# Gated cross-attention on one core: how the context matrix is loaded and transposed, and how W_mem's columns are read

## The chip, the core and the metric

The kernel runs on one core of a Trainium2 chip. The metric is the device time of one execution in microseconds. Before the change it is 992.16 us, the median of three runs (992.13 to 992.58). Engines are named as in the profile: PE is the tensor engine (PEld its weight loads), DVE the vector engine, ACT the scalar engine, POOL GpSimd, SP the engine that here only issues DMAs.

## The reference

Inputs are `x` (8 x 1024 x 1024), a context `mem` (8 x 64 x 512), `W_mem` (1024 x 512), `W_gate` (1024 x 2048), a bias and a norm weight, all float32. Cut to what is computed:

```python
memory_proj = jnp.einsum('bme,de->bmd', memory, W_mem)
scores = jnp.einsum('bnd,bmd->bnm', hidden_states, memory_proj) / jnp.sqrt(jnp.float32(D))
attn = jax.nn.softmax(scores, axis=-1)
memory_context = jnp.einsum('bnm,bmd->bnd', attn, memory_proj)
gate_input = jnp.concatenate([hidden_states, memory_context], axis=-1)
gate = jax.nn.sigmoid(jnp.einsum('bnf,df->bnd', gate_input, W_gate) + b_gate)
fused = hidden_states + gate * memory_context
return _rmsnorm(fused, norm_w)
```

The change concerns the first line alone: the product of the context with W_mem. Here B = 8, M = 64 and E = 512, so the context is 512 rows (`BM`) of 512 numbers; D = 1024.

## The kernel before, in words

The kernel has an opening, which is the part that matters here, and a long main loop.

**The order of the work.** Nearly every instruction is kept in program order on its engine (`pin`, line 88). A helper `load` (line 96) issues a DMA on SP, so all of these stand in one queue. A DMA or an instruction waits until the tile that it writes is free and the tiles that it reads are written; tiles of one tag share a buffer.

**The opening.** PE first multiplies a tile of zeros nine times (`pz`, lines 118 to 120). Meanwhile the context comes into two tiles `memq`, 256 rows each, in eight DMAs of pieces of 512 bytes: each DMA fills 32 partitions with a quarter of the columns (`load_mem`, lines 130 to 132). With the columns spread over four groups of partitions in this way, a block-wise transpose of 32x32 on DVE gives the full transpose; `transpose_mem` (lines 190 to 196) does this in four instructions, reading every fourth element (`chunks`, line 106), into `memT`, which has the 512 columns on partitions in four chunks of 128 and the 512 rows along the free dimension. W_mem arrives transposed in `wm` (line 128): two quarters by ACT's queue (line 137), the last half by SP (line 139). ACT then copies it into `wmp` (lines 199 to 209), which turns columns that lie eight elements apart into contiguous ones, in eight copies of 128x512.

**The product.** Eight PSUM banks `pm` (lines 226 to 228) take D in eight chunks `j`, each 128 rows of D by 512 context rows, and lines 229 to 239 accumulate over the four chunks `k` of E. For k = 0 the product is done in two halves of 256 columns, so that it can begin with the first half of the context; for the other k each matmul has 512 columns. A float32 matmul appears as two records of PE, each with a weight load of its own. DVE copies the eight banks to `mpT` (line 241), and PE goes on with the context's share of the gate, `pg` (lines 433 to 454: eight tiles, each of eight matmuls of 512 columns), fed by the eight tiles `w2`.

**Queues around it.** SP issues, in this order: the context, the last half of W_mem, the eight `w2` tiles, the bias, the two `w1` tiles, the first block of x (`load_xq(0)`, line 242, four DMAs), the norm weight, then 16 stores of the transposed projection to `mgd` (line 253) and four to `mpd` (line 260), and later the stores of the `pg` stages (line 441). `xq` has the same buffer as `wm` (tag "xq"). At most eight of these DMAs are under way at once. The first reader of `xq` is `transpose_x` in the list `first` (line 425), which is begun in the fifth `pg` tile (line 446).

**The main loop.** For each of 16 blocks of 512 rows of x, seven outer products of a Strassen-like scheme, each in seven inner products (`kA` to `kF`), with scores, softmax and gate between them by slots. The change doesn't touch it.

Of the kernel before, what the change touches and what calls it, by code (L numbers as in the profile page):

```python
# [8 lines left out]
F32 = mybir.dt.float32  # L9
# [6 lines left out]
P = 128  # L16
# [4 lines left out]
def tile_gated_cross_attention_rmsnorm(  # L21
# [41 lines left out]
    nc = tc.nc  # L63
    B, N, D = x.shape
    M, E = mem.shape[1:]
# [3 lines left out]
    BM = B * M  # L69
    KD = D // P  # L70
    KE = E // P
    H = 512
    C = 256
# [7 lines left out]
    apool = ctx.enter_context(tc.tile_pool(name="apool", bufs=1))  # L81
    rot = ctx.enter_context(tc.tile_pool(name="rot", bufs=2))
    small = ctx.enter_context(tc.tile_pool(name="small", bufs=1))
    ps = ctx.enter_context(tc.tile_pool(name="ps", bufs=1, space=PSUM))
    ps_ctx = ctx.enter_context(tc.tile_pool(name="ps_ctx", bufs=2, space=PSUM))
    dram = ctx.enter_context(tc.tile_pool(name="dram", bufs=1, space=DRAM))

    pin = tc.keep_in_program_order

    def mm(o, lhsT, rhs, start, stop):  # L90
        pin(nc.tensor.matmul(o, lhsT, rhs, start=start, stop=stop, skip_group_check=True))  # L91
# [4 lines left out]
    def load(o, i):  # L96
        pin(nc.sync.dma_start(o, i))

    def t4k(pool, shape, tag, name):
        return pool.tile(shape, F32, tag=tag, name=name)  # L100

    def rows_by_chunk(w, n):

        return w.rearrange("(p j) f -> p j f", j=n)

    def chunks(t, n):

        return t.rearrange("p s e -> p (s e)").rearrange("p (m j) -> p j m", j=n)
# [3 lines left out]
    def bank(n, shape, name):  # L112
        return ps.tile(shape, F32, tag=banks[n % 5], name=name)
# [1 line left out]

    zeros = t4k(small, [P, C], "junk", "zeros")
    pin(nc.vector.memset(zeros, 0.0))
    pz = ps.tile([P, C], F32, tag="sc", name="pz")
    for _ in range(9):
        mm(pz, zeros[:, :P], zeros, True, True)  # L120

    memq = [t4k(rot, [P, BM // 64, E // 4], "l2", f"memq{i}") for i in range(2)]
    memr = mem.rearrange("b m e -> (b m) e").rearrange(
        "(g s c) (i e) -> g i c s e", g=2, c=32, i=4
    )
    wm = t4k(xqpool, [P, KE, D], "xq", "wm")

    def load_mem(g):  # L130
        for i in range(4):
            load(memq[g][32 * i : 32 * (i + 1), :, :], memr[g, i])

    wmr = rows_by_chunk(w_mem_t, KE)
    load_mem(0)
    for k in range(2):
        pin(nc.scalar.dma_start(wm[:, k, :], wmr[:, k, :]))
    load_mem(1)
    load(wm[:, 2:, :], wmr[:, 2:, :])
    w2r = rows_by_chunk(w_gate_t[D:, :], KD)  # L140
    w2 = []
    for k in range(KD):
        t = t4k(*((gpool, [P, D], "gate") if k < 7 else (apool, [P, D], "s4")), f"w2_{k}")
# [36 lines left out]
    ident = const.tile([P, P], F32, name="ident")  # L180
# [6 lines left out]
    mgd = dram.tile([2, BM, D], F32, name="mgd")  # L187
    memT = [t4k(apool, [P, 2, BM], f"a1{i + 1}", f"memT{i}") for i in range(2)]

    def transpose_mem(g, i):  # L190
        pin(
            nc.vector.transpose(
                memT[i][:, :, g * (BM // 2) : (g + 1) * (BM // 2)],
                chunks(memq[g], KE)[:, 2 * i : 2 * i + 2],
            )
        )


    wmp = []
    for k in range(KE):  # L200
        t = t4k(apool, [P, KD, P], ("a21", "a22", "s1", "s2")[k], f"wmp{k}")
        for j in (0, KD // 2):
            pin(
                nc.scalar.copy(
                    t[:, j : j + KD // 2, :],
                    chunks(wm[:, k : k + 1, :], KD)[:, j : j + KD // 2],
                )
            )
        wmp.append(t)

    for i in range(2):
        for g in range(2):
            transpose_mem(g, i)

    mpT = [
        t4k(rot, [P, 2, BM], tag, f"mpT_{tag}_{i}")
# [6 lines left out]


    mpq = [t4k(apool, [P, 4, Q4], f"a{i}{j}", f"mpq{i}{j}") for i in (1, 2) for j in (1, 2)]
    pm = [bank(j, [P, BM], f"pm{j}") for j in range(5)]
    pm += [ps_ctx.tile([P, BM], F32, tag="ctx", name=f"pm{j}") for j in (5, 6)]
    pm += [ps.tile([P, BM], F32, tag="sc", name="pm7")]
    for k in range(KE):

        for cols in ([slice(0, BM // 2), slice(BM // 2, BM)] if k == 0 else [slice(0, BM)]):
            for j in range(KD):
                mm(
                    pm[j][:, cols],
                    wmp[k][:, j, :],
                    memT[k // 2][:, k % 2, cols],
                    k == 0 and cols.start == 0,
                    k == KE - 1,
                )
    for j in range(KD):  # L240
        pin(nc.vector.tensor_copy(mpT[j // 2][:, j % 2, :], pm[j]))
    load_xq(0)
# [189 lines left out]
    done, n = 0, 0  # L432
    for h in range(2):
        cols = slice(h * H, (h + 1) * H)
# [349 lines left out]
```

## Time and profile before

| what | value |
|---|---|
| median of three runs | 992.16 us (992.13 to 992.58) |
| the profiled execution's own time | 992.3 us |
| its span | 990.5 us, mean granted clock 0.995 |
| busy: PE, DVE, POOL, ACT | 972.9, 812.2, 688.7, 327.9 us |
| chain that ended last: PE, DVE, DMA | 95%, 2%, 1% |
| first record of `pm`, first record of `pg` | 11.43, 40.70 us |
| ACT copies `wmp<-wm` (8) | 8.4 us |
| DVE transposes `memT<-memq` (4) | 4.2 us |

The profile shows one execution. The span goes from its first to its last instruction; 1.8 us of the execution's time lie around it. A group of instructions is written as line, engine, operation, output<-inputs by the program's names, shapes and count, then busy time and the mean of one in ns, then the idle time of the engine just before them and what ended it. The matmuls and DMAs have the lines of their helpers (91 and 97), so one goes by the names of tiles. The chain of work is followed back from the last instruction to what released each step. PE's records overlap each other, since matmuls are pipelined: what counts is the distance from start to start.

### The profile page before, as it was taken

The page shows a single profiled execution, that of the slowest core. Times are in us where ns is not written, and L with a number is a line of the kernel's source. Part 1 is how long each engine was busy: PE and PEld are TensorE (multiplying, and loading weights), DVE is VectorE, ACT ScalarE, POOL GpSimd, SP SyncE. Part 2 cuts the span into 40 slices and gives each one's busy share as a digit, 9 for nine tenths or more (in the row PEclk, how much of TensorE's full clock was granted, in tenths as well). Part 3 has the DMA queues.
Part 4 walks back from the last instruction along what each step waited for, and adds up shares of the span by engine and source line. Part 5 has one row for each costly group of instructions (what it writes and reads, how often), then busy time and mean ns, then how long its engine had stood idle before and what let it go on. Part 6 is the DMA issues. An engine that isn't in the chain of part 4 may idle for free.

```text
span 990.5 us, 14285 instructions
## 1 busy us (share of the span) xinstructions
PE 972.9 (98%) x4962; PEld 768.9 (78%) x4962; DVE 812.2 (82%) x1491; ACT 327.9 (33%) x596; POOL 688.7 (70%) x851
## 2 busy tenths in 40 slices
PE   7999999999999999999999999999999999999995
PEld 5445888888788888888888888888887888888873
DVE  1587787979898897979788897979798988979787
ACT  3000215234343416143333425152343434161444
POOL 0002677878788787878697886878787887878772
PEclk9999999999999999999999999999999999999998
DMA  9951628192825547291926456381927365381612
GB/s 313 308 184 47 114 40 185 43 197 81 153 93 120 136 106 161 60 195 65 175 91 118 118 127 140 82 195 43 186 81 142 114 127 118 89 188 60 176 65 85
DMA packets 70792, 126.76 MB, mean 128 GB/s; under 512 B 12480, under 2 KB 49344, under 8 KB 70336
## 3 DMA queue, kind: packets, MB, share of 16 engines
q1 hardware_dynamic: 61792, 93.34, 35.1%
q0 software_dynamic: 8640, 31.46, 17.1%
q10 hardware_dynamic: 288, 1.05, 0.4%
q8 instruction: 39, 0.64, 0.3%
q14 instruction: 33, 0.27, 0.1%
HBM read 85.98 MB, written 39.85 MB: 127 GB/s over the span
## 4 chain that ended last, share of the span: by engine, by line
PE 95%; DVE 2%; DMA 1%; issue 0%; ACT 0%; POOL 0%; SPq 0%; DVEq 0%; ACTq 0%
PE kA L91 19%; PE pc L91 12%; PE kE L91 11%; PE kF L91 10%; PE kD L91 10%; PE kC L91 10%; PE kB L91 10%; PE psT L91 6%; PE pg L91 6%; PE pm L91 3%; DVE gate L94 1%; DMA memq<-in_mem 1%; DVE gate L598 0%; PE pa L395 0%; PE sc L369 0%
## 5 line engine op out<-in xcount | busy, mean ns | idle before, releaser
L94 POOL TENSOR_TENSOR gate<-gate,u 128x256 f32<-128x256 f32 x336 | 270.6, 836 | 122.5 <-DVE u L94 120.5
L94 POOL TENSOR_TENSOR l<-a 128x256 f32<-128x256 f32 x128 | 129.1, 1009 | 153.7 <-PE pg L91 89.4
L520 ACT ACTIVATE gate<-gate 128x512 f32<-128x512 f32 x128 | 79.0, 629 | 400.5 <-DVE gate L94 400.5
L301 DVE STREAM_TRANSPOSE a<-xq 128x512 f32<-128x512 f32 x128 | 137.8, 1099 | 0.0
L91 PE MATMUL pc<-mg,attnT 64*128 64x256 f32 x512 | 127.4, 389 | 0.0
L549 DVE SCALAR_TENSOR_TENSOR gate<-gate,ss,nw_sb 128x512 f32<-128x512 f32 x120 | 125.2, 1053 | 1.1
L91 PE MATMUL kB<-it,l 128*128 128x256 f32 x448 | 115.0, 379 | 0.0
L91 PE MATMUL kD<-it,l 128*128 128x256 f32 x448 | 115.0, 379 | 0.0
L91 PEld LDWEIGHTS pc<-mg,attnT 64*128 64x128 f32 x512 | 90.6, 186 | 29.7 <-issue 21.2
L91 PE MATMUL kA<-w,a 128*128 128x256 f32 x384 | 98.7, 379 | 0.4 <-ACT u L664 0.4
L91 PEld LDWEIGHTS kD<-it,l 128*128 128x128 f32 x448 | 85.1, 190 | 11.6
L91 PEld LDWEIGHTS kB<-it,l 128*128 128x128 f32 x448 | 85.1, 190 | 11.6
L94 DVE TENSOR_TENSOR gate<-gate,pc 128x512 f32<-128x512 f32 x128 | 87.2, 681 | 5.9 <-ACT gate L520 5.9
L664 ACT COPY u<-kA 128x256 f32<-128x256 f32 x112 | 40.5, 362 | 138.4 <-PE kA L91 136.4
L91 PEld LDWEIGHTS kA<-w,a 128*128 128x128 f32 x384 | 71.6, 190 | 10.2 <-ACT u L664 0.8
L94 POOL TENSOR_TENSOR l<-s 128x256 f32<-128x256 f32 x96 | 75.6, 787 | 1.8 <-PE kF L91 1.8
L94 DVE TENSOR_TENSOR u<-u,kB 128x256 f32<-128x256 f32 x112 | 45.6, 407 | 30.3 <-PE kB L91 26.3
L91 PE MATMUL kE<-it,a 128*128 128x256 f32 x256 | 69.0, 392 | 0.0
L91 PE MATMUL kA<-t,s 128*128 128x256 f32 x256 | 67.4, 386 | 0.0
L91 PE MATMUL kC<-w,l 128*128 128x256 f32 x256 | 65.7, 379 | 0.0
L91 PE MATMUL kF<-w,l 128*128 128x256 f32 x256 | 65.7, 379 | 0.0
L534 ACT ACTIVATE junk<-gate 128x1024 f32<-128x1024 f32 x60 | 63.5, 1058 | 1.5 <-DMA gate<-in_x 0.4
(105 smaller groups left out, 1959.8 us busy)
## 6 DMA issues: line engine op xcount, KB each, us to landing
xq<-in_x SPq DMA_DIRECT2D x64, 512.0 KB, 10.1
gate<-in_x POOLq DMA_DIRECT2D x60, 512.0 KB, 9.0
out<-gate SPq DMA_DIRECT2D x60, 512.0 KB, 2.6
w<-in_w_gate_t SPq DMA_DIRECT2D x8, 512.0 KB, 9.5
w<-in_w_gate_t SPq DMA_DIRECT2D x2, 2048.0 KB, 17.2
mg<-mgd SPq DMA_DIRECT2D x16, 256.0 KB, 4.2
mgd<-mpq SPq DMA_DIRECT2D x16, 128.0 KB, 2.6
mgd<-g SPq DMA_DIRECT2D x8, 256.0 KB, 2.1
```

What stands on the lines that cost most here:

```text
L91: pin(nc.tensor.matmul(o, lhsT, rhs, start=start, stop=stop, skip_group_check=True))
L94: pin(eng.tensor_tensor(o, a, b, op))
L301: nc.vector.transpose(A[key][:, :, r * P : (r + 1) * P], chunks(xq[q][:, 4 * t : 4 * t + 4, :], KD)[:, half * KH : (half + 1) * KH],)
L520: pin(nc.scalar.activation(g, g, AF.Sigmoid))
L534: nc.scalar.activation(junk, O[q, t], AF.Square, accum_out=ss[:, t % 2 : t % 2 + 1])
L549: nc.vector.scalar_tensor_tensor(g[:, cols], g[:, cols], rstd[:, t % 2 : t % 2 + 1], nw_sb[:, cols], ALU.mult, ALU.mult,)
L664: pin(nc.scalar.copy(p1, kb["A"]))
```

## The change

The context comes in two plain loads of 256 rows, two rows of 2 KB to a partition, both on SP. It is transposed on PE, 16 blocks of 128x128: the block, with every fourth element of a row, is the stationary operand, the identity the moving one. The blocks go to four PSUM banks `pt`, one for each chunk of E; DVE and ACT copy them to `memT` in turn, 256 columns at a time. The four banks are those that the product takes last (`pm4` to `pm7`). After the transposes of each half of the context come that half's products of chunk k = 0 for the first four chunks of D; when both halves are done, the other four chunks follow for k = 0 with 512 columns, and then the rest.

W_mem's columns, eight elements apart, are read from `wm` as the stationary operand as they lie; `wmp` and its copies are gone. With that `wm` is read until the product's last matmul. ACT's queue issues only W_mem's first quarter; the second goes to SP behind the context. The warm-up has five products of zeros instead of nine, in another bank.

```diff
@@ -115,27 +115,19 @@
     zeros = t4k(small, [P, C], "junk", "zeros")
     pin(nc.vector.memset(zeros, 0.0))
-    pz = ps.tile([P, C], F32, tag="sc", name="pz")
-    for _ in range(9):
+    pz = bank(0, [P, C], "pz")
+    for _ in range(5):
         mm(pz, zeros[:, :P], zeros, True, True)

-    memq = [t4k(rot, [P, BM // 64, E // 4], "l2", f"memq{i}") for i in range(2)]
-    memr = mem.rearrange("b m e -> (b m) e").rearrange(
-        "(g s c) (i e) -> g i c s e", g=2, c=32, i=4
-    )
+    memr = mem.rearrange("b m e -> (b m) e").rearrange("(g s p) e -> g p s e", g=2, p=P)
+    memq = [t4k(rot, [P, 2, E], "l2", f"memq{i}") for i in range(2)]
     wm = t4k(xqpool, [P, KE, D], "xq", "wm")
-
-    def load_mem(g):
-        for i in range(4):
-            load(memq[g][32 * i : 32 * (i + 1), :, :], memr[g, i])
-
     wmr = rows_by_chunk(w_mem_t, KE)
-    load_mem(0)
-    for k in range(2):
-        pin(nc.scalar.dma_start(wm[:, k, :], wmr[:, k, :]))
-    load_mem(1)
+    pin(nc.scalar.dma_start(wm[:, 0, :], wmr[:, 0, :]))
+    for g in range(2):
+        load(memq[g], memr[g])
+    load(wm[:, 1, :], wmr[:, 1, :])
     load(wm[:, 2:, :], wmr[:, 2:, :])
@@ -187,30 +179,21 @@
-    def transpose_mem(g, i):
-        pin(
-            nc.vector.transpose(
-                memT[i][:, :, g * (BM // 2) : (g + 1) * (BM // 2)],
-                chunks(memq[g], KE)[:, 2 * i : 2 * i + 2],
-            )
-        )
-
-
-    wmp = []
-    for k in range(KE):
-        t = t4k(apool, [P, KD, P], ("a21", "a22", "s1", "s2")[k], f"wmp{k}")
-        for j in (0, KD // 2):
-            pin(
-                nc.scalar.copy(
-                    t[:, j : j + KD // 2, :],
-                    chunks(wm[:, k : k + 1, :], KD)[:, j : j + KD // 2],
+    def transpose_mem(g):
+
+        cols = slice(g * (BM // 2), (g + 1) * (BM // 2))
+        for k in range(KE):
+            for r in range(2):
+                n = 2 * g + r
+                pin(
+                    nc.tensor.transpose(
+                        pt[k][:, n * P : (n + 1) * P],
+                        chunks(memq[g][:, r : r + 1, :], KE)[:, k],
+                        ident,
+                    )
                 )
-            )
-        wmp.append(t)
-
-    for i in range(2):
-        for g in range(2):
-            transpose_mem(g, i)
+            o = memT[k // 2][:, k % 2, cols]
+            pin((nc.scalar.copy if k % 2 else nc.vector.tensor_copy)(o, pt[k][:, cols]))
@@ -223,20 +206,33 @@
-    pm = [bank(j, [P, BM], f"pm{j}") for j in range(5)]
+    pt = [bank(4, [P, BM], "pt0")]
+    pt += [ps_ctx.tile([P, BM], F32, tag="ctx", name=f"pt{k}") for k in (1, 2)]
+    pt += [ps.tile([P, BM], F32, tag="sc", name="pt3")]
+    pm = [bank(j, [P, BM], f"pm{j}") for j in range(4)]
+
+    def mem_product(j, k, cols=slice(0, BM)):
+        mm(
+            pm[j][:, cols],
+            chunks(wm[:, k : k + 1, :], KD)[:, j],
+            memT[k // 2][:, k % 2, cols],
+            k == 0 and cols.start == 0,
+            k == KE - 1,
+        )
+
+    for g in range(2):
+        transpose_mem(g)
+        for j in range(KD // 2):
+            mem_product(j, 0, slice(g * (BM // 2), (g + 1) * (BM // 2)))
+    pm.append(bank(4, [P, BM], "pm4"))
     pm += [ps_ctx.tile([P, BM], F32, tag="ctx", name=f"pm{j}") for j in (5, 6)]
     pm += [ps.tile([P, BM], F32, tag="sc", name="pm7")]
-    for k in range(KE):
-
-        for cols in ([slice(0, BM // 2), slice(BM // 2, BM)] if k == 0 else [slice(0, BM)]):
-            for j in range(KD):
-                mm(
-                    pm[j][:, cols],
-                    wmp[k][:, j, :],
-                    memT[k // 2][:, k % 2, cols],
-                    k == 0 and cols.start == 0,
-                    k == KE - 1,
-                )
+    for j in range(KD // 2, KD):
+        mem_product(j, 0)
+    for k in range(1, KE):
+        for j in range(KD):
+            mem_product(j, k)
```

## The prediction

> **What bounds the kernel now.** I read the shares of busy time and the chain of work first, then who waited for whom, then the opening by stages. On the page the tensor engine (PE) has 98% of the span and 95% of the chain. Over the whole run, who waited for whom leaves it three waits:
>
> ```profile
> PE pm L91 <- DVE memT L192: 4.3, 1, 4.3
> PE kA L91 <- ACT u L664: 1.6, 3, 1.1
> PE pz L91 <- DVE zeros L117: 1.2, 1, 1.2
> ```
>
> The columns are us in total, times, longest. After its first product (`pm`, W_mem times mem) PE hardly stops, so whatever makes `pg`, the product behind `pm`, start earlier moves the end by as much. The chain of work in order of time (start, us, what) shows what sets that start:
>
> ```profile
> 2.17 7.89 DMA memq<-in_mem
> ...
> 10.18 1.11 DVE memT L192
> 11.29 0.14 issue
> 11.43 29.43 PE pm L91 x80
> 40.86 39.48 PE pg L91 x92
> ```
>
> The mem load lands at 10.06, VectorE (DVE) transposes for 1.1 us, PE starts at 11.43. The operations in order of time put the first `pg` record at 40.70, which I use below. The stages (start:end, length, then busy us and records of PE, PEld, DVE, ACT, POOL, then granted clock, DMA share, GB/s) show two handicaps more:
>
> ```profile
> 0.00:2.00 2.00, 0.80 (x2) 0.71 (x3) 0.27 (x1) 0.31 (x1) 0.74 (x7) 1.00 0.01 2
> 2.00:10.00 8.00, 5.12 (x17) 3.88 (x16) 0.00 (x0) 4.16 (x5) 0.00 (x0) 1.00 1.07 242
> ...
> 12.00:14.70 2.70, 2.70 (x7) 2.11 (x7) 2.37 (x3) 0.00 (x0) 0.00 (x0) 0.50 1.00 410
> 15.20:20.00 4.80, 4.80 (x24) 4.23 (x23) 0.18 (x1) 3.79 (x4) 0.00 (x0) 1.00 1.03 411
> 20.20:40.60 20.40, 20.40 (x49) 9.02 (x48) 4.71 (x7) 0.00 (x0) 0.00 (x0) 1.00 1.05 358
> ```
>
> The DMA engines are full from 2 us on, yet move 242 GB/s while mem comes in pieces of 512 bytes, against 411 with whole rows. And `pm` begins at half clock. From these rows a record (one of the two passes of a float32 matmul) of 256 columns takes 0.216 us, of 512 columns 0.429 us. `pm` has 32 of the first and 48 of the second: 6.9 + 20.6 = 27.5 us; it took 40.70 - 11.43 = 29.3, so the slow clock cost 1.8.
>
> [...] two transposes back to back, below, start 0.11 us apart. [...] clock 0.50 at 12 to 14.7 us, after 4.3 us of idle PE. [...] The trace has no strided weight load, but ScalarE reads `wm` with 32-byte steps:
>
> ```profile
> L520 ACT ACTIVATE gate<-gate 128x512 f32<-128x512 f32 x128 | 79.0, 629 | 400.5 <-DVE gate L94 400.5
> L534 ACT ACTIVATE junk<-gate 128x1024 f32<-128x1024 f32 x60 | 63.5, 1058 | 1.5 <-DMA gate<-in_x 0.4
> ...
> L204 ACT COPY wmp<-wm 128x512 f32<-128x512 f32 x8 | 8.4, 1114 | 7.6 <-DMA wm<-in_w_mem_t 7.6
> ```
>
> Contiguous: (1058 - 629)/512 = 0.84 ns an element and 200 ns fixed. Strided: (1114 - 200)/512 = 1.79 ns, 2.1 times as much.
>
> **The change part by part.**
>
> *Loads.* Eight mem pieces of 512-byte runs become two loads of 2 KB runs; W_mem's second quarter goes from ACT's queue to SP's, behind them. The first quarter (0.52 MB) and the first mem half (0.52 MB) share the 16 engines: 1.05 MB from 2.0 us. At 242 GB/s that is 4.3 us, at 411 it is 2.6; I take 330, between the two: 3.2, plus an estimated half us for the slowest engine and the semaphore, and 0.1 to wake PE. **First transpose at 5.8 us** (5.2 to 6.6). Nearest row: W_mem's first quarter lands 5.3 us after its issue at 0.74, so at 6.1, amid small packets. The second mem half, 0.52 MB more, comes some 1.6 us later, at about 7.4, and is wanted at 9.5. W_mem's second quarter follows at about 9, wanted near 16.6; the last half at about 12, wanted near 23.5. All are hidden.
>
> *Transposes on PE.* Sixteen are added to PE. The contiguous kind:
>
> ```profile
> 107.20 0.38 PE L369 MATMUL sc<-ident,sT 128*128 128x128 f32 x2
> ```
>
> with 0.272 us each, so 0.38 - 0.27 = 0.11 from start to start, which is also all a contiguous weight load needs. The strided load is unknown. Call its time from start to start L. Below 0.11 it can't go, since the identity must still stream through. Above, I have no firm end; three times the contiguous is 0.33. I take ScalarE's ratio: 128 x 1.79 = 0.23. Sixteen transposes: 16 x 0.23 = 3.7 us, all on the path, eight before each half product.
>
> *Copies out of PSUM.* Eight of 128x256, half on ACT (362 ns, the row of `u<-kA`), half on DVE (about 410 ns, the sums that read a `k` bank). Only the first of each group is waited for, and it runs under the remaining six transposes (6 x 0.23 = 1.4 us): zero. If L is 0.11 that cover is 0.7 and about 0.15 us shows per group. The banks handed on to `pm4`..`pm7` are emptied under the half products: zero.
>
> *Product.* Eight half matmuls (16 records of 256), then 56 records of 512: the same 27.5 us of streaming, but a strided weight load before each. Beside 0.429 a load of 0.23 is hidden; beside 0.216 it shows: 16 x 0.23 = 3.7 instead of 3.5.
>
> *Removed.* Four DVE transposes (4.2 us; the first is on the path) and eight ACT copies (8.4 us, under the mem load): their worth is in the start time. Four warm-up products fewer: five end near 5.3, when the transposes are about due, so the clock should stay up. That the zeros tile and the warm-up's bank come free earlier is worth nothing: their next users come later.
>
> *What gets later.* wm's buffer is now free only when the last `pm` matmul has read it, so `load_xq(0)`, four DMAs on SP, issues at about 37 instead of 20. Behind it on SP stand `nw_sb`, 16 stores to `mgd`, four to `mpd` and those of the `pg` stages. Today the four xq loads land at 41.6 to 49.1 anyway, behind w1; issued at 37 they land around 50. Their first reader:
>
> ```profile
> 78.97 2.08 DVE L301 STREAM_TRANSPOSE a<-xq 128x512 f32<-128x512 f32 x2
> ```
>
> That becomes about 75.5: 25 us of cover. The stores keep their absolute times: the first `pg` store still lands at about 62, and the DVE operation that needs its buffer, four tiles of 6.9 us into `pg`, moves from 68 to 65. Cover 3 us; PE has five banks more. w2 (landed by 25) and w1 (by 39, first read at 49.5) arrive no later than now. Zero. POOL's queue is untouched. After `pm`, `pg` and the rest follow as before.
>
> *Sum.* 5.8 + 3.7 (transposes) + 3.7 (half products) + 56 x 0.429 (24.0) = 37.2 for the first `pg` record, against 40.7: **3.5 us earlier**. The same by terms: start 5.6 earlier, slow clock 1.8 gone, transposes 3.7 and slow halves 0.2 added. The profiled execution took 992.3 (span 990.5, 1.8 around it); the median of the runs is 992.16. So 988.8 for it and **988.7** for the median.
>
> **Rivals.**
> - *Strided loads cost nothing extra* (L = 0.11): 5.8 + 1.8 + 0.3 + 3.5 + 24.0 = 35.4, gain 5.3: 986.9. For it: DVE transposes of 128x512 take 1.08 us with 16-byte steps and 1.10 with 32-byte steps, so step length alone does nothing there; against it: ScalarE's 2.1.
> - *Strided loads are far slower than ScalarE's*: this one ends slower than before. It sits in the weight loads of the transposes and of all 72 `pm` records. Up to 0.429 the stage costs 5.8 + 32L + 24.0; that equals 40.7 at L = 0.34, the point from which it decides. Past 0.429 every record pays: at L = 0.45 it is 5.8 + 88 x 0.45 = 45.4, 4.7 us later: 996.9.
> - *The clock falls*: [...] Price as today, 1.8: 990.5. [...] Against it: less than 3 us pass between the warm-up and the first half product.
> - *The first load is late*: two rings share the engines and the start is unsteady; at 8.0 us the gain is 1.3: 990.9.
>
> **How the numbers follow.** Forecast (L near 0.2 to 0.27) 0.50; no penalty 0.20; slower loads 0.12; clock 0.11; late load 0.07. A measurement can tell about 0.2%, 2.0 us. Forecast and no penalty give faster, 0.70; clock and late load lie within 2.0 us, and a part of the slow loads (L 0.28 to 0.40) too: same 0.20; slower 0.10. The range goes from the free load with a start at 5.2 (986.3) to past clock and late load (991.5), leaving out most of the slow-load case.
>
> **What would show it.** First transposes at 5.2 to 6.6; pitch of transposes about 0.23; half records at 0.22 to 0.25, full ones still 0.429; clock 1.0 throughout `pm`; first `pg` near 37; no PE wait between `pg` and the first `kA`. Wrong if `pm` records of 512 are spaced more than 0.43, or if PE waits later for `xq`.

## The result, and the profile after

The changed kernel takes 989.31 us, the median of six runs (989.2 to 990.88), against 992.28 for six runs of the kernel before (992.13 to 992.58): a ratio of 0.9974, 95% interval 0.9961 to 0.9987, so 3.0 us or 0.3% less. The times of the changed kernel fall into two groups, four of 989.2 to 989.3 and two of 990.6 to 990.9. The profiled execution is one of the upper group: 990.88 us, span 989.1.

First the chain of work of the changed kernel over its first 80 us (start, us, what), to be held against the one in the prediction:

```profile
0.75 5.79 DMA memq<-in_mem
6.54 0.14 issue
6.67 1.95 PE pt L189 x8
8.62 2.88 PE pm L91 x8
11.50 0.96 PE pt L189 x8
12.46 26.11 PE pm L91 x64
38.58 41.63 PE pg L91 x97
```

The DVE transpose is gone from the chain, and PE's work on the context starts at 6.67 instead of 11.43. The next view is PE's work in order of time (start, us, engine, line, operation, names, shapes, count), first in this execution:

```profile
1.20 4.63 PE L91 MATMUL pz<-zeros 128*128 128x256 f32 x10 [1.20 <-DVE zeros L117]
6.67 1.95 PE L189 MATMUL pt<-ident,memq 128*128 128x128 f32 x8 [0.84 <-DMA memq<-in_mem]
8.42 3.08 PE L91 MATMUL pm<-memT,wm 128*128 128x256 f32 x8
11.34 1.13 PE L189 MATMUL pt<-ident,memq 128*128 128x128 f32 x8
12.30 26.28 PE L91 MATMUL pm<-memT,wm 128*128 128x256 f32 x64
38.42 1.88 PE L91 MATMUL pg<-w,mpT_l 128*128 128x512 f32 x4
```

and then in a later run ("six more DMAs", below), which has the same PE instructions up to here and fell into the lower group:

```profile
1.19 4.36 PE L91 MATMUL pz<-zeros 128*128 128x256 f32 x10 [1.19 <-DVE zeros L117]
6.62 1.21 PE L193 MATMUL pt<-ident,memq 128*128 128x128 f32 x8 [1.07 <-DMA memq<-in_mem]
7.67 2.24 PE L91 MATMUL pm<-memT,wm 128*128 128x256 f32 x8
9.75 1.13 PE L193 MATMUL pt<-ident,memq 128*128 128x128 f32 x8
10.71 26.28 PE L91 MATMUL pm<-memT,wm 128*128 128x256 f32 x64
36.83 1.45 PE L91 MATMUL pg<-w,mpT_l 128*128 128x512 f32 x3
```

Both start within about 0.05 us of each other, and both need the same time from the second group of transposes on. Between them lie only the first eight transposes (1.95 against 1.21) and the first eight half records, those of 256 columns (3.08 against 2.24): in the first execution they run at half clock, all but the last two of the half records, in the second at full clock. That is 1.6 us at the first `pg` record. The stages view gives a granted clock of 1.00 from the start in both; it knows nothing before the first change of clock that the trace holds (10.79 and 5.14 us here), so here the spacing of the records is what tells the clock: half records come every 0.427 us at half clock, every 0.237 to 0.240 at full clock.

The waits of PE over the whole run (us, times, longest) have one new row in place of the old 4.3:

```profile
PE kA L91 <- ACT u L660: 1.6, 3, 1.1
PE pz L91 <- DVE zeros L117: 1.2, 1, 1.2
PE pt L189 <- DMA memq<-in_mem: 0.8, 1, 0.8
```

From the first `pg` record to the last block of the main loop every PE record is 2.28 us earlier than before, and the last one of all still 2.25. The span ends only 1.43 earlier: 0.82 us are lost behind PE's last record.

### The profile page after: what moved, and what is told of

Its sections match the earlier page's. It is cut to its first block, busy times and chain, and to the rows that moved or that the text cites. A ratio compares the mean times of both kernels' runs of the same rounds, so it can differ in the third digit from the quotient of the medians.

```text
span 989.1 us, 14267 instructions
## 1 busy us (share of the span) xinstructions
PE 974.1 (98%) x4962; PEld 775.8 (78%) x4962; DVE 810.3 (82%) x1491; ACT 321.7 (33%) x592; POOL 688.1 (70%) x851
## 4 chain that ended last, share of the span: by engine, by line
PE 96%; DVE 2%; DMA 1%; issue 0%; ACT 0%; POOL 0%; DVEq 0%; ACTq 0%
PE kA L91 19%; PE pc L91 12%; PE kE L91 11%; PE kF L91 10%; PE kD L91 10%; PE kC L91 10%; PE kB L91 10%; PE psT L91 6%; PE pg L91 6%; PE pm L91 3%; DVE gate L94 1%; DMA memq<-in_mem 1%; DVE gate L594 0%; PE pa L391 0%; PE sc L365 0%
```

## The experiments

The ratio given with each is to the kernel before, timed beside it. In these longer series the kernel before itself shows three groups of times, near 990.5, 992.2 and 993.5, with a median of 992.2 each time.

**W_mem's first quarter behind the first half of mem** (against the changed kernel):

```diff
-    pin(nc.scalar.dma_start(wm[:, 0, :], wmr[:, 0, :]))
-    for g in range(2):
-        load(memq[g], memr[g])
+    load(memq[0], memr[0])
+    load(wm[:, 0, :], wmr[:, 0, :])
+    load(memq[1], memr[1])
```

> The changed kernel with one thing moved: W_mem's first quarter is loaded by SP between the two halves of mem, not by ACT beside the first half. Theory (the first transpose waits because the first half of mem shares the 16 DMA engines with W_mem's first quarter): the half lands 1.2 to 1.4 us earlier, at 5.2 to 5.4 instead of 6.54; the quarter lands near 6.6 and is wanted only after eight transposes, near 6.4 to 7; first record of pg about 1 us earlier at the same clock; time near 988.3. Rival (the landing is set by a fixed way from issue to semaphore, not by shared bytes): the half still lands after 6.2, time near 989.3.

Measured 988.44 (ratio 0.996, 0.9947 to 0.9972). The row of the tile `memq` says how long its two DMAs take from issue to landing; first for the changed kernel, then here:

```profile
DMA to landing us min/median/max: 5.8/6.2/6.6
```

```profile
DMA to landing us min/median/max: 3.9/5.3/6.6
```

The shortest is the first half: 5.8 us against 3.9, so it lands at 4.65 instead of 6.54. The theory holds, and by more than expected (the quarter also changes from ACT's queue to SP's, but the bytes account for it): 0.85 MB had moved by this landing, against 1.43 MB by the landing in the changed kernel, at nearly the same rate (322 GB/s from 2 us on, against 303). The transposes start only at 5.62, because the warm-up still occupies PE until then, and the first `pg` record comes 0.85 earlier than at 36.83:

```profile
5.62 1.44 PE L189 MATMUL pt<-ident,memq 128*128 128x128 f32 x8
35.98 1.45 PE L91 MATMUL pg<-w,mpT_l 128*128 128x512 f32 x3
```

**Nine warm-up products again** (against the changed kernel):

```diff
-    for _ in range(5):
+    for _ in range(9):
         mm(pz, zeros[:, :P], zeros, True, True)
```

> The changed kernel with nine warm-up products again instead of five. Theory ([...]): the clock is full at every pm record, so the half products of the first group of mem come every 0.24 us, not 0.43; the warm-up ends between 7.0 and 8.3 and holds the transposes back by 0.4 to 1.6 us; all times lie between 989.3 and 990.8. Rival (the two groups come from something else, the end of the kernel or the loads): the two groups stay 1.4 us apart though the clock is full at the first pm record.

Measured 989.71 (0.9978, 0.9968 to 0.9987), times from 989.34 to 990.71. In the profiled execution the clock is full from 5.22 and all half records come every 0.24 us; the transposes start at 7.16, 0.7 us after their data. All as expected, but it decides nothing against the rival: times near 989.5 (six) and near 990.5 (three) both occur, and only an execution of the first kind was profiled. No gain from it.

The traces say more on the clock. In the kernel before the recorded clock rises at 4.82 us (to 1.00), falls at 11.65 (to 0.50) and rises again at 15.06: 6.83 and 3.41 apart, as if it were set anew every 3.41 us; in all eleven traces it stays up from the last rise for a whole number of such steps (284 to 286), and falls behind PE's last record (at 980.17 in the changed kernel, whose last record ends at 977.86). Counted back from the rise at 10.79 in the changed kernel, PE is at work for 2.77 us of the step from 0.55 to 3.96, for 2.57 us of the next, and throughout the third, at whose end the clock rises. In the execution with six more DMAs the step from 1.73 to 5.14 is full, and the clock rises at its end; in the four other profiled executions with five warm-up products it rises between 5.27 and 6.36. So where the steps happen to fall seems to decide whether ten records of warm-up are enough. This is read from the traces; no run moved the steps.

**The copies taken out alone** (against the kernel before):

```diff
-    wmp = []
-    for k in range(KE):
...
-        wmp.append(t)
...
-                    wmp[k][:, j, :],
+                    chunks(wm[:, k : k + 1, :], KD)[:, j],
```

> One half of the change alone: the kernel before, with its loads, its warm-up and its transposes on DVE, but W_mem's columns read with stride from wm; the eight ACT copies are gone. Theory (the copies lie under the mem load; a strided weight load shows beside 256 columns alone): first pm record still at 11.4, each of the 32 records of 256 columns at full clock 0.02 us slower, 0.4 to 0.7 us in all, records of 512 unchanged at 0.429; time 992.5 to 993.0. Rival (the copies held up the product): pm starts earlier or runs faster, time below 991.5. Second rival (strided loads also lengthen the records of 512): more than 1 us slower.

Measured 993.01 (1.0008, 1.0000 to 1.0017), 0.84 above the kernel before, at the upper end of what was expected. `pm` starts at 11.16 and its records of 256 come every 0.237 to 0.240 us, those of 512 every 0.429. The first `pg` record follows 28.47 us after the first of `pm`, against 27.58 for copied columns at the same clock (the last experiment). The copies were hidden, and reading with stride only costs.

**The new loads and PE transposes with the copies kept** (against the changed kernel; `copy_wm` holds the two ACT copies of a quarter as in the kernel before):

```diff
-            chunks(wm[:, k : k + 1, :], KD)[:, j],
+            wmp[k][:, j, :],
...
+    copy_wm(0)
     for g in range(2):
         transpose_mem(g)
...
+    for k in range(1, KE):
+        copy_wm(k)
```

> The other half of the change alone: the new loads, the transposes on PE and the warm-up of five, but W_mem's columns still copied by ACT, the first quarter ahead of the copies out of PSUM and the others behind them. Theory (the gain lies in the earlier start alone): first transpose at 6.5 to 6.8 as in the changed kernel, records of 256 at 0.216 instead of 0.238, 0.3 us less; the copies of the first quarter end near 7.9 and may hold back the first half product by some tenths; time within 0.6 us of the changed kernel. Rival (reading with stride, not the loads, makes the gain): time near 992.3.

Measured 988.98 (0.9967, 0.9955 to 0.998): 0.3 below the changed kernel. First transpose at 6.70, half records every 0.216. The gain lies in the loads, the transposes and the warm-up, which no run takes apart; the copies' removal gives a little of it back.

**Six more DMAs** (against the changed kernel):

```diff
-        load(w1[h], rows_by_chunk(w_gate_t[:D, :], KD)[:, 4 * h : 4 * h + 4, :])
+        for c in range(4):
+            load(
+                w1[h][:, c : c + 1, :],
+                rows_by_chunk(w_gate_t[:D, :], KD)[:, 4 * h + c : 4 * h + c + 1, :],
+            )
```

> The changed kernel with the two w1 loads split into eight, so that the program issues as many hardware DMAs as the kernel before (the change took six away). Theory (the end is 0.8 us longer in the changed kernel because the completion semaphores are handed out in turn, and with six DMAs fewer the last store gets one that SP waits for second among eight pairs, not last): the stretch from the last store's landing to the end of the span is back from 1.73 to about 0.91 us, PE's records stay as in the changed kernel, all times fall by 0.8, to near 988.5 (and 989.9 where the clock comes up late). Rival (the longer end comes from the length of the program or from chance): the stretch stays at 1.7, times as in the changed kernel.

Measured 988.42 (0.9965, 0.9952 to 0.9979): four times of 988.3 to 988.4 and one of 989.8, both 0.9 below the groups of the changed kernel. In the traces of the kernel before and the changed one the DMAs of SP and ACT take eight semaphores in turn, and at the end of the program SP waits for all of them, one instruction after another; the last store's is the eighth of these waits before and the second in the changed kernel. The rows below count SP's instructions on that line from the moment at which the last store has landed (ns shortest/median/longest, then the first and the last start); in the changed kernel from 987.38 to 988.0,

```profile
L776 SPq EVENT_SEMAPHORE  x7: 27/28/28, 987.4 to 987.8; - x7
L776 SPq DRAIN  x1: 7/7/7, 987.9 to 987.9; - x1
```

in the kernel before from 989.62 to 989.8,

```profile
L780 SPq DRAIN  x2: 7/7/7, 989.7 to 989.8; - x2
L780 SPq EVENT_SEMAPHORE  x1: 28/28/28, 989.6 to 989.6; - x1
```

and in this run from 985.71 to 985.86:

```profile
L780 SPq DRAIN  x2: 7/7/7, 985.8 to 985.9; - x2
L780 SPq EVENT_SEMAPHORE  x1: 28/28/28, 985.7 to 985.7; - x1
```

Of the seven waits of the changed kernel the first is for the last store; six others stand behind it, until 987.8, and the second drain follows only at 988.2. Before and in this run, the last store's semaphore is the last to be waited for. With six DMAs more the stretch from the landing to the end of the span is 0.92 us again, against 1.73. It is 0.91 to 0.92 in all five profiles of kernels that issue 268 DMAs and 1.72 to 1.74 in all six of kernels that issue 262, whatever the length of the run: the number of DMAs sets it. Why the second drain comes 0.34 us after the first, and not 0.06, stays open.

**All products in halves** (against the changed kernel):

```diff
     for k in range(1, KE):
         for j in range(KD):
-            mem_product(j, k)
+            for g in range(2):
+                mem_product(j, k, slice(g * (BM // 2), (g + 1) * (BM // 2)))
```

> The changed kernel with the products of the other three chunks of E in halves of 256 columns too: 96 records of 256 in place of 48 of 512. Theory (a strided weight load needs 0.238 us and lies hidden only under records of 512): every record of 256 comes 0.238 after the one before, 96 x 0.238 - 48 x 0.429 = 2.3 us more, first pg record 2.3 later, time 2.3 above the changed kernel. Rival (stride costs nothing once the loads run ahead of the products; the 0.238 at the start has another cause): 0.216, 0.1 us more.

Measured 991.57 (0.9999, 0.9991 to 1.0007), 2.26 above the changed kernel. The stage from 18 to 38 us, `pm` alone (columns as in the prediction, without ACT and POOL):

```profile
18.00:38.00 20.00, 20.00 (x85) 20.00 (x85) 3.97 (x6) 1.00 0.71 295
```

PEld is busy all the time, 20.00 of 20.00 us, and from start to start a record takes 0.237 to 0.240 us, not 0.216 (the 85 include those that the edges cut): the weight loads set the pace. Under the changed kernel's records of 512 they don't: from 14.8 to 38.4 us PEld is busy for 17.11 of 23.60, and a record takes 0.429.

**Neighbouring columns of W_mem** (against the changed kernel; the projection's columns come in another order, so the output differs):

```diff
-            chunks(wm[:, k : k + 1, :], KD)[:, j],
+            wm[:, k, j * P : (j + 1) * P],
```

> The changed kernel with W_mem's stationary blocks taken as 128 neighbouring columns instead of every eighth. This computes the projection with its columns in another order, so the output is not the reference's; every size and count is the same. Theory (only the weight loads beside 256 columns show the stride): the 16 records of 256 come every 0.216 instead of 0.238, 0.35 us less, weight loads shown with 0.19 instead of 0.31 to 0.34, records of 512 at 0.429 as before; time 0.3 to 0.4 below the changed kernel in the same clock state. Rival (stride slows the moving operand too): records of 512 get shorter, over 1 us less.

Measured 988.64 (0.9964, 0.9952 to 0.9977). The weight loads of `pm` (ns shortest/median/longest), changed kernel and this one:

```profile
L91 PEld LDWEIGHTS pm<-memT,wm x72: 312/314/338, 8.2 to 37.6; 128*128 128x128 f32 x72
```

```profile
L91 PEld LDWEIGHTS pm<-memT,wm x72: 186/190/190, 7.6 to 35.4; 128*128 128x128 f32 x72
```

Half records come every 0.216, those of 512 every 0.429 as ever. The first `pg` record is at 36.24, 0.59 earlier than in the execution of the same clock above, not 0.35: the first record after each group of transposes also loses 0.13 us (0.395 against 0.269 to the next record). By the rows above its weight load is 0.12 us longer with the stride (0.312 against 0.190); that the 0.13 is this load, uncovered, is an estimate from those two figures, and no run isolates it.

**What these point to, together** (against the changed kernel; not shown are the loads of the first experiment, four warm-up products and the split w1 loads):

```diff
-    wmr = rows_by_chunk(w_mem_t, KE)
+    wmr = w_mem_t.rearrange("(j p) f -> p j f", p=P)
...
-                        chunks(memq[g][:, r : r + 1, :], KE)[:, k],
+                        memq[g][:, r, k * P : (k + 1) * P],
```

> What the runs so far point to, put together: W_mem's first quarter behind the first half of mem; four warm-up products, ending near 4.8 when that half lands; mem's blocks transposed from 128 neighbouring columns, with W_mem's rows loaded to match; the w1 loads split, so that the last store's semaphore is waited for last. Theory: first transpose at 4.7 to 5.0 (5.62 in the kernel with W_mem's quarter moved, held there by the warm-up), transposes every 0.109 at full clock, wait for W_mem's quarter until about 6.4, end 0.8 shorter; 1.0 to 1.8 below the kernel with the quarter moved: 986.6 to 987.4. Rival (each part takes its own gain from the others, since the first half product waits for W_mem's quarter near 6.5 in any case): only the shorter end remains, 987.6. A third way: with a shorter warm-up the clock comes up later, and 1 to 1.5 us are lost in part of the executions.

Measured 987.08, from 986.87 to 987.55 (0.9949, 0.9937 to 0.9962): 2.2 below the changed kernel, the best of all. PE's opening:

```profile
1.19 3.78 PE L91 MATMUL pz<-zeros 128*128 128x256 f32 x8 [1.19 <-DVE zeros L117]
4.80 1.17 PE L193 MATMUL pt<-ident,memq 128*128 128x128 f32 x8
6.08 2.25 PE L91 MATMUL pm<-memT,wm 128*128 128x256 f32 x8
8.16 1.04 PE L193 MATMUL pt<-ident,memq 128*128 128x128 f32 x8
9.06 26.34 PE L91 MATMUL pm<-memT,wm 128*128 128x256 f32 x64
35.24 2.31 PE L91 MATMUL pg<-w,mpT_l 128*128 128x512 f32 x5
```

The parts add up: the first `pg` record is 0.74 earlier than with the moved quarter alone, and the stretch behind the last landing is 0.91 us. The half product does wait for W_mem's quarter (0.3 us, landed at 5.94). Transposes of neighbouring columns come every 0.109. No time lies high in five runs, so the third way was not seen.

**The kernel before with 18 warm-up products:**

```diff
-    for _ in range(9):
+    for _ in range(18):
         mm(pz, zeros[:, :P], zeros, True, True)
```

> The kernel before with 18 warm-up products instead of nine, which keep PE at work until about 10.9 us, just ahead of the first pm record at 11.4; nothing else. Theory (part of the change's gain is the clock alone: the kernel before leaves PE idle from 7 to 11.4 and begins pm at half clock in most executions): pm starts at 11.2 to 11.5 at full clock, 0.216 from the first record, first pg near 38.9 to 39.1 instead of 40.7; most times near 990.5, the lowest group of the kernel before, so that 1.7 of the 3.0 us between the medians need no other loads or transposes. Rival (the groups of times have another cause, or the longer warm-up delays pm when the clock comes up late): times spread as before around 992.2, or above.

Measured 990.68, all 21 runs from 990.38 to 991.24 (0.9984, 0.9978 to 0.9991), while the kernel before ran from 990.39 to 993.64 beside it. PE's opening:

```profile
1.19 9.66 PE L91 MATMUL pz<-zeros 128*128 128x256 f32 x36 [1.19 <-DVE zeros L117]
11.28 27.75 PE L91 MATMUL pm<-memT,wmp 128*128 128x256 f32 x80 [0.43 <-DVE memT L192]
38.86 3.60 PE L91 MATMUL pg<-w,mpT_l 128*128 128x512 f32 x8
```

`pm` takes 27.75 us where it took 29.43, from nearly the same start (11.28 and 11.43). The recorded mean granted clocks of the kernel before go with its groups: 0.997 near 990.5, 0.994 to 0.996 near 992.2, 0.992 to 0.994 near 993.5. So the two upper groups are the clock, though only one of the 992.2 group has a profile, and about 1.6 of the 3.0 us between the medians are to be had with one number. What decides the group fits the steps of 3.41 us: in the profiled execution PE was at work for 0.22 us of the step from 8.23 to 11.65, and the clock fell. Without the copies (third experiment) PE idled 3.3 us, but across two steps (6.25 to 9.67 and 9.67 to 13.08) with 1.58 and 1.92 us of work, and the clock stayed up.

## Why the prediction was right, point by point

It gave 988.7 with a range of 986.3 to 991.5; the median is 989.31. 3.5 us were forecast, 3.0 measured. The mechanism is right: an earlier start of PE, paid for with transposes on PE. But sizes on both sides were off and cancelled in part: that the number came so close is in part luck. Against the lower group the start was 0.8 late, the half products took 0.5 and the end 0.8 more than counted, and the transposes gave 1.7 back. Times in us, the predicted sum against the profiled execution and the one of the lower group shown above (which has the six DMAs more):

| term | predicted | profiled | lower group |
|---|---|---|---|
| first transpose starts | 5.8 | 6.67 | 6.62 |
| first eight transposes | 1.84 | 1.75 | 1.05 |
| first half products | 1.84 | 2.92 | 2.07 |
| next eight transposes | 1.84 | 0.96 | 0.97 |
| next half products | 1.84 | 2.06 | 2.07 |
| 56 records of 512 | 24.0 | 24.06 | 24.05 |
| first `pg` record | 37.2 | 38.42 | 36.83 |
| from it to the end of the span | 949.8 (as before) | 950.7 | 949.8 |

- **Loads.** "First transpose at 5.8 us (5.2 to 6.6)" was mis-sized by 0.9 and just outside its own bounds. The half us for the slowest engine and the semaphore was the author's estimate, taken from no row; here the sixteen parts of this load land from 5.51 to 6.54. The rate was not far off: 330 GB/s from 2.0 us on were taken, 303 measured up to the landing at 6.54. The bytes were: the sum counted 1.05 MB, but 1.43 MB had moved by then, since part of the second half of mem, next in SP's queue, moved before the first half was complete. What the sharing with W_mem's first quarter costs, which the sum did count, is shown by the run that moves the quarter: the half lands at 4.65, 1.9 us earlier.
- **Transposes on PE.** "I take ScalarE's ratio" held for the products, whose stationary operand has steps of 32 bytes, and not for the transposes, with 16: there the rival without a penalty was nearly right. At full clock the transposes come every 0.122 us, against 0.109 with neighbouring columns, not 0.23. At half clock they come every 0.213. The traces show two costs, but on two kinds of instruction; whether the step or the kind makes the difference, no run here decides.
- **Product.** The half records are at 0.237 to 0.240 (0.23 forecast), the records of 512 unchanged, both confirmed by the runs in halves and with neighbouring columns. The 0.13 at the head of each group was not counted.
- **The clock.** "Five end near 5.3 ... so the clock should stay up" is the step that failed. In the profiled execution there was nothing to stay up: the warm-up records come every 0.427 us to the last, and the clock rises for the first time at 10.79. And "slow clock 1.8 gone" counted as a gain something that the kernel before loses in most executions but not in all: its lowest group, at 990.5, lacks it. The rival "the clock falls", given 0.11, came true by its effect in two of six executions, with 1.4 to 1.6 us in place of 1.8, but not by its mechanism: the clock did not fall behind the warm-up, it had not risen. Why it had not, no run isolates; PE was idle for 0.84 us between the end of the warm-up (5.83) and the first transpose (6.67).
- **Copies out of PSUM, banks, removed copies.** Zero, as said: PE has no wait for `memT` or a bank. Keeping the ACT copies of W_mem costs nothing and saves 0.3.
- **What gets later.** `xq` is issued at 38.6 and landed by 51.7; DVE reads it at 76.7, without a wait: zero, as said. But "The stores keep their absolute times" failed: behind xq on SP the first `pg` store lands at 65.2, not 62, and the DVE operation that needs its buffer starts at 66.1. Of the cover of 3 us 0.9 is left.
- **After `pm`.** "`pg` and the rest follow as before" holds for PE to 0.03 us, not for the end: 0.8 us for the turn of the semaphores, which the count of DMAs sets. It was not in the sum at all.

Of the signs that were named, the half records, the full ones and the missing PE wait came as said; the start (6.67 or 6.62), the pitch of the transposes and, in the profiled execution, the clock did not.

So in the lower group 3.9 us are won at `pg` and 0.8 given back at the end. Of the 3.9, 1.7 are the half clock that the profiled execution of before suffered (29.3 us from the first `pm` to the first `pg` record, 27.6 with 18 warm-up products), and 2.2 are the earlier start (4.8) less the transposes (2.0) and the stride (0.6). In the profiled execution, of the upper group, 2.3 are won at `pg`.

## What to carry to other kernels

Where a first product waits for data, ask what else is on the DMA engines in those few us, and let the transfer that is wanted first go alone; here a quarter of W_mem that is wanted some 2 us later held the first one back by 1.9 us. A strided stationary operand was free here under a moving operand of 512 columns (0.429 us a record with and without the stride), not under one of 256 (0.237 to 0.240 against 0.216), and copies that lie under a wait are not worth removing (taking them out alone cost 0.84 us). When a queue gets longer, look at the stores behind it too (the first of them landed at 65.2 instead of 62). Where PE idles ahead of its first real product, fill the gap to the end: that alone took 1.6 us off the kernel before, half of what the change seemed to give.

## What was not expected of the hardware

- Weight loads of 128 float32 columns need, from start to start, at most 0.110 us contiguous (transposes), 0.122 with steps of 16 bytes (transposes), 0.237 to 0.240 with steps of 32 bytes (products): 0.012 more in the one case, about double in the other. ScalarE's copy at 32 bytes shows nearly the same factor, 2.1.
- Which semaphore the last store got was worth 0.8 us at the end of the program: 1.73 against 0.92 us from the landing to the end of the span.
- Ten records of warm-up, from 1.2 us to 5.8 in one execution and to 5.6 in another of the same PE program, didn't bring the clock up reliably: full clock at 10.79 in the one and at 5.14 in the other. The changes of clock lay whole multiples of 3.41 us apart, and what PE did in each such step went with them: up after full ones (7.37 to 10.79 and 1.73 to 5.14), not after ones with 2.77 and 2.57 us of work, down after one with 0.22.
